# Moving the item product from GpSimd to VectorE and setting the AUGRU widths step by step, in a two-pass recurrent recommendation kernel

## The chip, the cores and the metric

The kernel runs on one NeuronCore of one Trainium2 chip. The metric is the device time of one launch in microseconds (us), the median of several runs. The engines are called as the profile calls them: PE is TensorE, DVE is VectorE, ACT is ScalarE, POOL is GpSimd, and SP is SyncE, which issues most of the DMAs. A matrix product on PE is preceded by a weight load, which the profile lists apart as PEld.

## The reference

There are 1024 items (`B`), 100 steps (`T`) and vectors of 128 numbers, all float32. A GRU runs over the history of every item; an attention network scores each hidden state against the item's embedding; the softmax over the steps pools the hidden states; a second recurrence, the AUGRU, runs over the hidden states with gates that the pooled values scale; and its output at the item's last step goes into a small network.

```python
def gru_step(h, x_t):                                   # 100 steps, all 1024 items
    r = sigmoid(i_r + h_r); z = sigmoid(i_z + h_z)      # i = x Wih' + bih, h = h Whh' + bhh
    n = tanh(i_n + r * h_n)
    return (1 - z) * n + z * h
keys = gru_seq                                          # (1024, 100, 128)
feat = concat([keys, q, keys - q, q * keys])            # q is the item's embedding
score = mlp(feat, [80, 40, 1], relu); score[mask != 1] = -inf
attn = softmax(score, axis=1)
pooled = einsum('bt,btd->bd', attn, keys)
att_seq = pooled.T[:T]
def augru_step(h, (x_t, a_t)):                          # x_t = keys[:, t], a_t = att_seq
    r = sigmoid([h, x_t] Wr' + br); u = a_t * sigmoid([h, x_t] Wu' + bu)
    h_hat = tanh([h * r, x_t] Wh' + bh)
    return (1 - u) * h + u * h_hat
attention_feature = aug_out[item, sequential_length - 1]
out = mlp([user, item, hist_sum, item * hist_sum, attention_feature], [200, 80, 1], sigmoid)
```

`hist_sum` is the masked sum of the history divided by the length. `sequential_length` is drawn uniformly from 1 to 100. Only the AUGRU output at the last step of an item is used, so an item needs no AUGRU step beyond its length.

## The kernel before

**Layout.** Hidden states lie with the 128 features on the partitions and the items on the free axis. The items are cut into two halves of 512 (`HB`), and everything is done half by half, so that one half's chain of elementwise work lies beside the other half's matrix products. A float32 product of 128x512 is two PE instructions in the trace.

**First phase (`gru_phase`).** A loop over the 100 steps; at each step, for each half: load the inputs of two steps ahead (`load`, `load_mask`; the tiles `x` and `m` have 8 buffers each), the GRU step (`gru`, lines 354 to 398), the attention of the previous step (`attend`, lines 418 to 435), the transposition of the previous hidden state for the keys in memory (`transpose`), one stage of the softmax if a block of steps is complete (`stage`), the masked history sum (`history`, lines 350 and 351) and up to two additions to the pooled sum (`pool`, lines 511 to 526). After the second half, `attend_more` does the second and third attention layers of both halves (`px`, lines 618 and 627).

The work lies on the engines so. PE: for each half and step, the gates (`ps`, line 363, 12 instructions), the first attention layer (`pm`, four instructions: line 431 with the hidden state `hn`, line 432 with the product `kq` of `hn` and the item's embedding), and four transposes (`pk`, line 409). DVE: the elementwise chain of the GRU, `u` (383), `ps` plus `u` (393), `d` (396, 397), `hn` (398), and the sum `f` of `pm` and a constant (434). ACT: the sigmoids and tanh (375, 380, 394), the copy of the transposed keys (410), the ReLUs (435, 627). POOL: the item product `kq` (429), the history (`xm`, `hist`) and the pooled sum (`kw`, `pooled`, with the softmax weights `e`).

The tiles `pm`, `pk`, `px` and `pt` (the transposed scores) share two PSUM buffers in turn, so `px` needs the buffer that `f` sets free.

**Order.** The order of the instructions on each engine is fixed when the kernel is built: a scheduler places every instruction by its own estimate of when its inputs are ready, and each engine then runs its list strictly in that order. What stands in the list behind a waiting instruction waits too.

**Between the phases.** The items are ranked by their lengths (`rank`), and sorted weights and row numbers are made, so that in the second phase the items stand in order of falling length, alternating between the halves. In the first phase the kernel also counts how many items are alive at each step (`count`) and compares this with a table of widths: `over` tells whether an item would fall outside it.

**Second phase (`augru_phase`).** The 100 AUGRU steps, for each half six products with 128 columns of weights (lines 725 and 727), three activations, five DVE operations (735 to 745) and the transposition of the key (`pk`, 714, one instruction for each 128 items), all on the first `w` items of the half only. The keys come by indirect DMAs in quarters of four steps (`load_rows`, `G = 4`). `widths` holds one width for each of the 25 groups of four steps: `RAGGED`, 512 for the first three groups and then falling by 21 per group to 52. If `over` is 1 the phase runs with `FULL`, 512 everywhere. The program holds both versions one after the other, and every engine branches on `over`. When a block of 128 items falls out of the width, `predict` computes its outputs, and an indirect DMA writes them.

Of the kernel before, what the change touches and what calls it, by code (L numbers as in the profile page):

```python
# [18 lines left out]
P = 128  # L19
B = 1024  # L20
T = 100
HB = 512
NH = B // HB
NG = B // P
GH = HB // P
# [16 lines left out]
G = 4  # L42
NQ = T // G
# [1 line left out]
AHEAD = 2  # L45


FULL = [HB] * NQ
TOP, FALL = 556, 21
RAGGED = [min(HB, TOP - FALL * q) for q in range(NQ)]  # L50


@with_exitstack
def kernel(ctx: ExitStack, tc: tile.TileContext, a: dict, out: bass.AP):
# [16 lines left out]
    nc = tc.nc  # L71
# [6 lines left out]
    over_d = dram.tile([1, 1], I32, name="over_d")  # L78
# [31 lines left out]
    def load_rows(q, i, widths):  # L110

        r = mid.tile([P, GH, G * P], F32, tag="once", name="rows") if q == 0 else (
            rows["pool"].tile([P, GH, G * P], F32, name="rows")
        )
        for g in range(-(-widths[q] // P)):
            gather(r[:, g, :], keys_d[q], g, i)
        rows[q, i] = r

    def gru_phase(pools):
# [58 lines left out]
        def load_later():  # L178
# [26 lines left out]
                out=alive,  # L205
# [16 lines left out]
            room_i = pre.tile([1, NQ, G], I32, name="room_i")  # L222
            nc.gpsimd.iota(
                room_i, pattern=[[-2 * FALL, NQ], [0, G]], base=2 * TOP, channel_multiplier=0
            )
            room = pre.tile([1, T], F32, name="room")
            nc.vector.tensor_copy(room, room_i.rearrange("o q g -> o (q g)"))
            nc.vector.tensor_scalar_min(room, room, float(B))
            nc.vector.tensor_tensor(out=room, in0=count, in1=room, op=ALU.is_gt)
            over = pre.tile([1, 1], F32, name="over")  # L230
            nc.vector.tensor_reduce(over, room, AX.X, ALU.max)
            over_i = pre.tile([1, 1], I32, name="over_i")
            nc.vector.tensor_copy(over_i, over)
            nc.sync.dma_start(out=over_d, in_=over_i)
            yield

# [78 lines left out]
        class Half:  # L315
# [102 lines left out]
            def attend(self, t):  # L418

                i = self.i  # L420
                mv = wp.tile([P, HB], F32, name="mv", bufs=4)
                self.old, self.mv = self.mv, mv
                if t == T:
                    nc.gpsimd.memset(mv, 0.0)
                if t >= T:
                    return
                h = self.h[t]
                kq = wp.tile([P, HB], F32, name="kq")
                nc.gpsimd.tensor_mul(kq, h, item[:, self.cols])  # L429
                p = pa.tile([P, HB], F32, tag="a", name="pm")  # L430
                nc.tensor.matmul(p, lhsT=wk[i], rhs=h, start=True, stop=False)  # L431
                nc.tensor.matmul(p, lhsT=wkq[i], rhs=kq, start=False, stop=True)  # L432
                f = wp.tile([P, HB], F32, name="f")
                nc.vector.tensor_add(f, p, q0[:, self.cols])  # L434
                nc.scalar.activation(mv, f, AF.Relu)
# [246 lines left out]
            half.features()  # L682
        sort_weights()
        for i in range(NH):
            load_rows(0, i, FULL)

    def augru_phase(pools, widths):

# [8 lines left out]
        rows["pool"] = kp  # L697

        def load_att(t, i):
            w = widths[t // G]  # L700
            at = wp.tile([P, HB], F32, name="at", bufs=6)
            nc.sync.dma_start(
                out=at[:, :w], in_=att_d[i][t, :w].partition_broadcast(P)
            )
            att[t, i] = at

        def load_key(t, i):

            q, n = divmod(t, G)
            w = widths[q]  # L710
            r = rows[q, i]
            p = pa.tile([P, HB], F32, tag="a", name="pk3")
            for g in range(-(-w // P)):
                nc.tensor.transpose(p[:, ts(g, P)], r[:, g, ts(n, P)], ident)  # L714
            k = wp.tile([P, HB], F32, name="k3", bufs=6)
            nc.scalar.copy(k[:, :w], p[:, :w])
            keys[t, i] = k

        def step(t, i):
            w = widths[t // G]  # L720
            k, at, h = keys.pop((t, i))[:, :w], att.pop((t, i))[:, :w], h3[i][:, :w]

            def gate(m, v, name):
                p = ps.tile([P, HB], F32, tag="g", name=name)[:, :w]
                nc.tensor.matmul(p, lhsT=m[:, 1, :], rhs=k, start=True, stop=v is None)
                if v is not None:
                    nc.tensor.matmul(p, lhsT=m[:, 0, :], rhs=v, start=False, stop=True)
                return p

            r = None  # L730
            if t:
                pr = gate(wr, h, "pr")
                r = wp.tile([P, HB], F32, name="r3")[:, :w]
                nc.scalar.activation(pr, pr, AF.Sigmoid, bias=later["br"])
                nc.vector.tensor_mul(r, h, pr)
            pu = gate(wu, h if t else None, "pu")
            nc.scalar.activation(pu, pu, AF.Sigmoid, bias=later["bu"])
            u = wp.tile([P, HB], F32, name="u3")[:, :w]
            nc.vector.tensor_mul(u, pu, at)
            ph = gate(wh, r, "ph")  # L740
            nc.scalar.activation(ph, ph, AF.Tanh, bias=later["bh"])  # L741
            if t:
                nc.vector.tensor_sub(ph, ph, h)  # L743
                nc.vector.tensor_mul(ph, u, ph)
                nc.vector.tensor_add(h, h, ph)
# [51 lines left out]
        for t in range(T):  # L797
            q, n = divmod(t, G)
            for i in range(NH):
                if n == 0 and 0 < q < NQ - 1:  # L800
                    load_rows(q + 1, i, widths)
                if t + 2 < T:
                    load_att(t + 2, i)
                if t + 1 < T:
                    load_key(t + 1, i)
                step(t, i)
            if n == G - 1:
                left = widths[q + 1] if q + 1 < NQ else 0
# [7 lines left out]
    over = nc.values_load(over_d, min_val=0, max_val=1)  # L816
    with tc.If(over > 0) as more:
        with ExitStack() as pools:
            augru_phase(pools, FULL)
    with more.Else():  # L820
        with ExitStack() as pools:
            augru_phase(pools, RAGGED)


# [64 lines left out]
```

## Time and profile before

| | us |
|---|---|
| median of 3 runs | 2664.23 (2659.52 to 2665.18) |
| profiled execution | 2684.05, its span 2681.6 |
| first phase: first `hn` to the start of the last | 15.5 to 1870.3 |
| second phase: first transposition of keys | 1932.5 |
| PE busy in the span | 2434.5 (91%) |
| POOL, DVE, ACT busy | 1370.2, 1382.1, 1215.7 |

A row of instruction groups gives the line, the engine, the operation and its tiles, the form, the count, the busy time and the mean of one in ns, and then the idle time of the engine ahead of these instructions with what ended it. A row of the timeline gives start and duration in us and, in brackets, the idle time of that engine just before with what ended it; `x2` means that two neighbours are merged into one row, so that the duration is that of both. The duration of a PE instruction contains its passage through the array; instructions that follow one another closely overlap, so what a step costs on PE is read from starts and not from durations.

### The profile page before, as it was taken

The numbers are of one execution on the slowest core, as the hardware profiler recorded it, in microseconds if no ns is written. First come the engines' busy times: TensorE is split into PE (matmuls) and PEld (weight loads), VectorE is DVE, ScalarE is ACT, GpSimd is POOL, SyncE is SP. The second block draws the span as 40 slices with busy tenths as digits, with TensorE's granted clock in tenths as the row PEclk, the third lists the DMA queues.
The fourth block names the chain that finished last, engine by engine and source line by source line (L and its number), as shares of the span: only waits on it lengthen the run. The fifth ranks groups of instructions, "written<-read, shape, count | busy, mean of one in ns | idle before, by whom it ended". The sixth has DMA issues, their size and how long they took to land. (4 is left out here: it accounts for less than half of the span.)

```text
span 2681.6 us, 25839 instructions
## 1 busy us (share of the span) xinstructions
PE 2434.5 (91%) x7688; PEld 1232.2 (46%) x7688; DVE 1382.1 (52%) x2530; ACT 1215.7 (45%) x2125; POOL 1370.2 (51%) x1215
## 2 busy tenths in 40 slices
PE   8999888898888888899888888897789999999998
PEld 3443333343333333344333333333444555667887
DVE  6644444544444444545444444454356666666664
ACT  3544444444444444444444444443234444455554
POOL 3457877565656767665656767667512111211220
PEclk9999999999999999999999999998799999999998
DMA  6323322212222222112222222111223233333331
GB/s 141 99 81 97 95 90 66 74 58 73 77 73 76 75 74 75 52 61 73 74 77 73 77 73 77 49 64 36 86 80 108 85 101 98 93 92 96 79 86 23
DMA packets 141655, 210.20 MB, mean 78 GB/s; under 512 B 29646, under 2 KB 75698, under 8 KB 141506
## 3 DMA queue, kind: packets, MB, share of 16 engines
q1 hardware_dynamic: 129410, 170.93, 20.7%
q0 software_dynamic: 12096, 37.54, 4.9%
q8 instruction: 62, 1.02, 0.2%
q14 instruction: 87, 0.71, 0.1%
HBM read 154.12 MB, written 53.87 MB: 78 GB/s over the span
## 5 line engine op out<-in xcount | busy, mean ns | idle before, releaser
L363 PE MATMUL ps<-x,wih 128*128 128x512 f32 x1200 | 603.2, 613 | 4.6 <-DMA x<-in_hist_x 4.6
L363 PE MATMUL ps<-hn,whh 128*128 128x512 f32 x1188 | 594.4, 609 | 0.0
L429 POOL TENSOR_TENSOR kq<-hn,item 128x512 f32<-128x512 f32 x200 | 254.5, 1278 | 559.1 <-DVE hn L398 540.5
L432 PE MATMUL pm<-kq,wkq 128*128 128x512 f32 x400 | 239.6, 684 | 190.2 <-POOL kq L429 190.1
L383 DVE SCALAR_TENSOR_TENSOR u<-ps,bhh,r 128x512 f32<-128x512 f32 x198 | 148.6, 750 | 506.2 <-ACT r L375 309.6
L101 POOL DMA_INDIRECT rows<-keys_d,idx x140 | 132.8, 949 | 535.9 <-PE pk L714 490.4
L363 PEld LDWEIGHTS ps<-hn,whh 128*128 128x128 f32 x1188 | 223.1, 195 | 326.8 <-issue 319.6
L410 ACT COPY kt<-pk 128x512 f32<-128x512 f32 x200 | 117.3, 586 | 517.2 <-PE pk L409 515.7
L363 PEld LDWEIGHTS ps<-x,wih 128*128 128x128 f32 x1200 | 221.7, 199 | 199.3 <-issue 197.9
L394 ACT ACTIVATE ps<-ps,bih 128x512 f32<-128x512 f32 x200 | 132.4, 662 | 321.6 <-DVE ps L393 317.9
L351 POOL TENSOR_TENSOR hist<-hist,xm 128x512 f32<-128x512 f32 x200 | 251.8, 1274 | 1.6
L434 DVE TENSOR_TENSOR f<-pm,q 128x512 f32<-128x512 f32 x200 | 136.7, 684 | 215.1 <-PE pm L432 215.0
L526 POOL TENSOR_TENSOR pooled<-pooled,kw 128x512 f32<-128x512 f32 x190 | 242.3, 1275 | 4.3
L350 POOL TENSOR_TENSOR xm<-x,m 128x512 f32<-128x512 f32 x200 | 229.4, 1162 | 22.9 <-DMA x<-in_hist_x 16.7
L432 PEld LDWEIGHTS pm<-kq,wkq 128*128 128x128 f32 x400 | 79.5, 210 | 300.1 <-POOL kq L429 223.6
L431 PE MATMUL pm<-hn,wk 128*128 128x512 f32 x400 | 206.9, 599 | 6.0 <-ACT kt L410 3.7
L396 DVE TENSOR_TENSOR d<-hn,ps 128x512 f32<-128x512 f32 x198 | 136.0, 687 | 138.5 <-ACT ps L394 137.6
L525 POOL TENSOR_TENSOR kw<-kt,e 128x512 f32<-128x512 f32 x190 | 196.8, 1052 | 1.7 <-DVE old L492 0.4
L409 PEld LDWEIGHTS pk<-ident,hn 128*128 128x128 f32 x800 | 112.6, 155 | 125.8 <-issue 116.8
L627 ACT ACTIVATE mv<-px,bx 41x512 f32<-41x512 f32 x202 | 137.9, 683 | 68.4 <-PE px L618 65.8
L375 ACT ACTIVATE r<-ps,brz 128x512 f32<-128x512 f32 x200 | 137.5, 688 | 67.7 <-PE ps L363 64.6
L743 DVE TENSOR_TENSOR ph<-ph,h 128x512 f32<-128x512 f32 (+22 forms) x198 | 94.6, 478 | 142.4 <-ACT ph L741 127.5
(139 smaller groups left out, 3608.7 us busy)
## 6 DMA issues: line engine op xcount, KB each, us to landing
x<-in_hist_x SPq DMA_DIRECT2D x212, 256.0 KB
keys_d<-kt SPq DMA_DIRECT2D x50, 1024.0 KB
m<-mask_d SPq DMA_DIRECT2D x200, 128.0 KB
at<-att_d SPq DMA_DIRECT2D x22, 256.0 KB
s_b<-mv SPq DMA_DIRECT2D x200, 2.0 KB
rows<-keys_d,idx POOLq DMA_INDIRECT x140
at<-att_d SPq DMA_DIRECT2D x8, 246.5 KB
at<-att_d SPq DMA_DIRECT2D x8, 236.0 KB
```

The costliest lines, as they stand in the source:

```text
L350: nc.gpsimd.tensor_mul(d, x, m)
L351: nc.gpsimd.tensor_add(acc, acc, d)
L363: nc.tensor.matmul(p, lhsT=w[:, g, :], rhs=v, start=(j == 0), stop=(j == len(parts) - 1),)
L375: nc.scalar.activation(r, pr, AF.Sigmoid, bias=brz[:, 0:1])
L383: nc.vector.scalar_tensor_tensor(out=u, in0=ph, scalar=bhh[:, 2:3], in1=r, op0=ALU.add, op1=ALU.mult,)
L429: nc.gpsimd.tensor_mul(kq, h, item[:, self.cols])
L431: nc.tensor.matmul(p, lhsT=wk[i], rhs=h, start=True, stop=False)
L432: nc.tensor.matmul(p, lhsT=wkq[i], rhs=kq, start=False, stop=True)
L434: nc.vector.tensor_add(f, p, q0[:, self.cols])
L525: eng.tensor_mul(d, k, w)
L526: eng.tensor_add(acc, acc, d)
L627: nc.scalar.activation(half.mv[r, :], p[r, :], AF.Relu, bias=bx[r, :])
```

## The change

The item product goes from `nc.gpsimd` to `nc.vector`. The width is looked up for each step and no longer for each group of four. There are three tables in place of two: a tight one, a wider one, and full width. In the tight one the width is 512 up to step 2 and then falls by 5.125 a step (rounded up to an even number) to 16; in the wider one it is 512 up to step 8 and falls in the same way to 46. The sum of the widths over the 100 steps is 30124 before, 26908 in the tight table and 29740 in the wider one. `over` is now 0, 1 or 2, the number of tables that some step does not fit, and the program holds three versions of the second phase behind two branches.

```diff
-FULL = [HB] * NQ
-TOP, FALL = 556, 21
-RAGGED = [min(HB, TOP - FALL * q) for q in range(NQ)]
+EIGHTH, FALL = 8, 41
+SPARE = (10, 40)
+ROOM = [[EIGHTH * (HB + n) - FALL * t for t in range(T)] for n in SPARE]
+WIDTHS = [[min(HB, 2 * -(-r // (2 * EIGHTH))) for r in room] for room in ROOM] + [[HB] * T]
...
-        for g in range(-(-widths[q] // P)):
+        for g in range(-(-widths[q * G] // P)):
             gather(r[:, g, :], keys_d[q], g, i)
...
+            over = pre.tile([1, len(SPARE)], F32, name="over")
+            for j, n in enumerate(SPARE):
+                room_i = pre.tile([1, T], I32, name="room_i")
+                nc.gpsimd.iota(
...
+                nc.vector.tensor_copy(room, room_i)
+                nc.vector.scalar_tensor_tensor(
...
+                nc.vector.tensor_reduce(over[:, j : j + 1], room, AX.X, ALU.max)
+            nc.vector.tensor_add(over[:, 0:1], over[:, 0:1], over[:, 1:2])
...
-                nc.gpsimd.tensor_mul(kq, h, item[:, self.cols])
+                nc.vector.tensor_mul(kq, h, item[:, self.cols])
...
-            w = widths[t // G]
+            w = widths[t]
...
-            if n == G - 1:
-                left = widths[q + 1] if q + 1 < NQ else 0
-                for g in range(GH):
-                    if left <= g * P < widths[q]:
-                        for i in range(NH):
-                            predict(g, i)
+            left = widths[t + 1] if t + 1 < T else 0
+            for g in range(GH):
+                if left <= g * P < widths[t]:
+                    for i in range(NH):
+                        predict(g, i)
...
-    with tc.If(over > 0) as more:
+    over = nc.values_load(over_d, min_val=0, max_val=len(SPARE))
+    with tc.If(over < 1) as fits:
+        augru(WIDTHS[0])
+    with fits.Else():
+        with tc.If(over < 2) as fits:
+            augru(WIDTHS[1])
+        with fits.Else():
+            augru(WIDTHS[2])
```

The lines below the tables stand one to sixteen lines later in the changed file; the same instruction is line 429 before and 441 after, for instance.

On POOL, in the middle of the first phase, this stood in the list of before. `e` are the softmax weights of a block, `kw` and `pooled` the pooled sum, `xm` and `hist` the history, `kq` the item product.

```order
L429 TENSOR_TENSOR kq<-hn,item 128x512 x6
L511 TENSOR_TENSOR pooled<-pooled,e 128x512
L525 TENSOR_TENSOR kw<-kt,e 128x512 x2
L526 TENSOR_TENSOR pooled<-pooled,kw 128x512 x2
L350 TENSOR_TENSOR xm<-x,m 128x512 x2
L351 TENSOR_TENSOR hist<-hist,xm 128x512 x2
L525 TENSOR_TENSOR kw<-kt,e 128x512 x2
L526 TENSOR_TENSOR pooled<-pooled,kw 128x512 x2
L350 TENSOR_TENSOR xm<-x,m 128x512 x2
L351 TENSOR_TENSOR hist<-hist,xm 128x512 x2
L525 TENSOR_TENSOR kw<-kt,e 128x512
L429 TENSOR_TENSOR kq<-hn,item 128x512
```

Six products stood in a row, then a whole block of pooling and history, and the seventh product behind it. In the changed list of POOL this place reads:

```order
L523 TENSOR_TENSOR pooled<-pooled,e 128x512
L537 TENSOR_TENSOR kw<-kt,e 128x512 x2
L538 TENSOR_TENSOR pooled<-pooled,kw 128x512 x2
L362 TENSOR_TENSOR xm<-x,m 128x512 x2
L363 TENSOR_TENSOR hist<-hist,xm 128x512 x2
L537 TENSOR_TENSOR kw<-kt,e 128x512 x2
```

The products are gone from it, and the rest of the order is nearly the same. On DVE, in the first phase, one half's turn was this before:

```order
L398 TENSOR_TENSOR hn<-ps_4879,d 128x512
L383 SCALAR_TENSOR_TENSOR u<-ps_4929,bhh,r 128x512
L393 TENSOR_TENSOR ps_4931<-ps_4931,u 128x512
L396 TENSOR_TENSOR d<-hn,ps_4931 128x512
L397 TENSOR_TENSOR d<-ps_4933,d 128x512
L398 TENSOR_TENSOR hn<-ps_4931,d 128x512
```

and in the changed list the end of one turn and the start of the next, with a stage of the softmax (`e`, `top`) in it, is this:

```order
L410 TENSOR_TENSOR hn<-ps_4830,d 128x512
L446 TENSOR_TENSOR f<-pm,q_173 128x512
L441 TENSOR_TENSOR kq<-hn,item 128x512
L487 TENSOR_TENSOR e<-pt,on 128x4x8
L488 TENSOR_REDUCE top<-e 128x4
L490 TENSOR_TENSOR top<-top 128x4
L491 TENSOR_TENSOR e<-top 128x4
L492 TENSOR_TENSOR e<-e,top 128x4x8
L395 SCALAR_TENSOR_TENSOR u<-ps_4883,bhh,r 128x512
```

The product now stands between `f` and the `u` of the other half. At the end of the second phase's first version, DVE has these rows before:

```order
L744 TENSOR_TENSOR ph<-u_17147,ph 128x512
L745 TENSOR_TENSOR h_1_99<-h_1_99,ph 128x512
L817 UNCONDITIONAL_BRANCH
L739 TENSOR_TENSOR u_17384<-pu,h_0_98 128x512
L747 TENSOR_TENSOR h_0_98<-u_17384,ph 128x512
```

and these in the changed list:

```order
L756 TENSOR_TENSOR ph<-u_16921,ph 128x16
L757 TENSOR_TENSOR h_1_99<-h_1_99,ph 128x16
L832 UNCONDITIONAL_BRANCH
L835 COMPARE_AND_BRANCH
L751 TENSOR_TENSOR u_17033<-pu,h_0_98 128x512
```

The version that stands first behind the branch was the full width (its last step is 512 wide); now it is the tight table (its last step is 16 wide). The first phase's list on PE, some 2060 rows, is the same but for one row.

More of the change, by code (lines that the diff above doesn't have):

```diff
@@ L221, in load_later @@
                 )
[L222 to L231, printed above, removed]
+            over = pre.tile([1, len(SPARE)], F32, name="over")
+            for j, n in enumerate(SPARE):
+                room_i = pre.tile([1, T], I32, name="room_i")
+                nc.gpsimd.iota(
+                    room_i,
+                    pattern=[[-NH * FALL, T]],
+                    base=NH * EIGHTH * (HB + n),
+                    channel_multiplier=0,
+                )
+                room = pre.tile([1, T], F32, name="room")
+                nc.vector.tensor_copy(room, room_i)
+                nc.vector.scalar_tensor_tensor(
+                    out=room,
+                    in0=count,
+                    scalar=float(EIGHTH),
+                    in1=room,
+                    op0=ALU.mult,
+                    op1=ALU.is_gt,
+                )
+                nc.vector.tensor_reduce(over[:, j : j + 1], room, AX.X, ALU.max)
+            nc.vector.tensor_add(over[:, 0:1], over[:, 0:1], over[:, 1:2])
             over_i = pre.tile([1, 1], I32, name="over_i")
-            nc.vector.tensor_copy(over_i, over)
+            nc.vector.tensor_copy(over_i, over[:, 0:1])
             nc.sync.dma_start(out=over_d, in_=over_i)
@@ L684, in gru_phase @@
         for i in range(NH):
-            load_rows(0, i, FULL)
+            load_rows(0, i, WIDTHS[-1])
     def augru_phase(pools, widths):
@@ L709, in load_key @@
             q, n = divmod(t, G)
-            w = widths[q]
+            w = widths[t]
             r = rows[q, i]
@@ L719, in step @@
         def step(t, i):
-            w = widths[t // G]
+            w = widths[t]
             k, at, h = keys.pop((t, i))[:, :w], att.pop((t, i))[:, :w], h3[i][:, :w]
@@ L806, in augru_phase, with augru @@
                 step(t, i)
-            if n == G - 1:
-                left = widths[q + 1] if q + 1 < NQ else 0
-                for g in range(GH):
-                    if left <= g * P < widths[q]:
-                        for i in range(NH):
-                            predict(g, i)
+            left = widths[t + 1] if t + 1 < T else 0
[3 more added lines that the diff above has]
+                        predict(g, i)
     with ExitStack() as pools:
         gru_phase(pools)
-    over = nc.values_load(over_d, min_val=0, max_val=1)
-    with tc.If(over > 0) as more:
+    def augru(widths):
         with ExitStack() as pools:
[L819 to L822, printed above, removed]
+            augru_phase(pools, widths)
+    over = nc.values_load(over_d, min_val=0, max_val=len(SPARE))
[6 more added lines that the diff above has]
+            augru(WIDTHS[2])
 def _laid_out(np, r):
```

## The prediction

> **What bounds the kernel now.** I first read the page's engine shares, then its groups.
>
> ```profile
> span 2681.6 us, 25839 instructions
> PE 2434.5 (91%) x7688; PEld 1232.2 (46%) x7688; DVE 1382.1 (52%) x2530; ACT 1215.7 (45%) x2125; POOL 1370.2 (51%) x1215
> ...
> L429 POOL TENSOR_TENSOR kq<-hn,item 128x512 f32<-128x512 f32 x200 | 254.5, 1278 | 559.1 <-DVE hn L398 540.5
> L432 PE MATMUL pm<-kq,wkq 128*128 128x512 f32 x400 | 239.6, 684 | 190.2 <-POOL kq L429 190.1
> ```
>
> PE carries both phases. Its one large idle time is the 190.1 us ahead of `pm`, line 432, for which POOL's item product is named; POOL itself idled 540.5 us waiting for `hn` ahead of that product. So POOL is not short of time: its list is in a bad order. The waits say how often, and the tile `hn` how long the phase is:
>
> ```profile
> PE pm L432 <- POOL kq L429: 190.1, 38, 7.5
> ```
>
> ```profile
> L398 DVE TENSOR_TENSOR hn<-ps,d x200: 671/692/694, 15.5 to 1870.3; 128x512 f32<-128x512 f32 x100
> ```
>
> 38 waits of up to 7.5 us; 1854.8 us for 99 steps, 18.7 us a step. The timeline of PE shows what a step would cost without them. `px` comes once a step, so the distance of two `px` is a step:
>
> ```profile
> 1015.17 1.06 PE L618 MATMUL px<-mv,w 121*41 121x512 f32 x4
> ...
> 1031.51 1.06 PE L618 MATMUL px<-mv,w 121*41 121x512 f32 x4
> ...
> 1051.48 1.06 PE L618 MATMUL px<-mv,w 121*41 121x512 f32 x4
> ...
> 1063.71 2.07 PE L432 MATMUL pm<-kq,wkq 128*128 128x512 f32 x2 [5.82 <-POOL kq L429]
> ...
> 1073.14 1.02 PE L432 MATMUL pm<-kq,wkq 128*128 128x512 f32 x2
> ...
> 1075.39 1.06 PE L618 MATMUL px<-mv,w 121*41 121x512 f32 x4
> ...
> 1091.19 1.06 PE L618 MATMUL px<-mv,w 121*41 121x512 f32 x4
> ```
>
> A clean step takes 15.80 us (1075.39 to 1091.19), one with a transposition of scores 16.34 (1015.17 to 1031.51), one with a wait of 5.82 us 23.91. The last is 8.11 over the clean one, 2.29 more than it waited: after the gap the pair of `pm` takes 2.07 us in place of 1.02, so the array runs at half speed for a while.
>
> The cause stands in POOL's timeline:
>
> ```profile
> 1025.65 1.06 POOL L511 TENSOR_TENSOR pooled<-pooled,e 128x512 f32<-128x512 f32 x1 [1.07 <-ACT e L485]
> 1026.67 2.05 POOL L525 TENSOR_TENSOR kw<-kt,e 128x512 f32<-128x512 f32 x2
> ...
> 1035.96 2.06 POOL L525 TENSOR_TENSOR kw<-kt,e 128x512 f32<-128x512 f32 x2
> ```
>
> Pooling and history run without a gap from 1025.65 to 1038.02 and on; the next product stands behind them, and PE waits.
>
> **Part 1: the product leaves POOL.** In the changed order no PE instruction of the loop waits for POOL's list. 99 steps of 15.80 are 1564 us, and 28 transpositions of scores (30 blocks in `ENDS`, two of them after the loop) at 0.54 add 15: 1579 against 1854.8, 275 less. About 10 of this is not POOL's: early on DVE waits for the lengths.
>
> ```profile
> 45.29 0.69 DVE L240 CAST order<-len_r 128x1024 f32<-128x1024 int32 x1 [9.55 <-DMA len_r<-in_len_i]
> ```
>
> So 265 us can go. The other way round: 190.1 less 6.34 after the loop (below) is 184 of idle time, and 37 times 2.29 is 85, together 269.
>
> After the last `hn` there is one more such wait, 6.34 us, worth 8.6 with its slow array:
>
> ```profile
> 1880.12 2.07 PE L432 MATMUL pm<-kq,wkq 128*128 128x512 f32 x2 [6.34 <-POOL kq L429]
> ```
>
> **Part 2: the product arrives on DVE.** The nearest row for its price is the same kind of product on DVE, two SBUF inputs of 128x512. Beside it stand three small DVE operations with two SBUF inputs, all of 128x4, at work while POOL did or did not run:
>
> ```profile
> L525 DVE TENSOR_TENSOR kw<-kt,e 128x512 f32<-128x512 f32 x8 | 5.5, 685 | 1.2 <-POOL pooled L526 1.2
> ```
>
> ```profile
> 1022.28 0.15 DVE L478 TENSOR_TENSOR top<-top 128x4 f32<-128x4 f32 x1
> ...
> 1025.72 1.01 DVE L492 TENSOR_TENSOR old<-den,e 128x4 f32<-128x4 f32 x1
> ...
> 1026.86 0.87 DVE L493 TENSOR_TENSOR den<-den,old 128x4 f32<-128x4 f32 x1
> ```
>
> 0.15 us with POOL idle, 1.01 and 0.87 with POOL at work: the DVE operation ends when POOL's current instruction ends (1025.72 + 1.01 is 1026.73, POOL's change from `pooled` to `kw`; 1026.86 + 0.87 is 1027.73, the middle of the two `kw`). So a product costs 0.69 us, and up to POOL's longest, 1.28, more: 1.97. How often POOL is at work follows from 150 us of the loop, 8 steps at 18.7:
>
> ```profile
> 1017.00:1167.00 150.00, 134.65 (x361) 58.83 (x360) 71.35 (x114) 67.50 (x103) 95.57 (x82) 0.93 0.22 71
> ```
>
> 95.57 us of POOL less 16 products of 1.28 are 75, of 8 steps of 15.9: 59%. The mean product should be about 0.69 + 0.6 x 0.64 = 1.1.
>
> The Trainium skill (GPSIMD Engine Reference, section Specifications) states that GpSimd's SBUF interfaces are shared with VectorE and contend with VectorE instructions of two SBUF inputs. That rule speaks against this change, and the rows above agree with it; read as one POOL instruction at a time it leaves the sum as it is, read as a lock for a whole run of POOL it is the first rival.
>
> What is behind the product in DVE's list is the other half's `u`. DVE idles ahead of it:
>
> ```profile
> 1078.69 0.75 DVE L383 SCALAR_TENSOR_TENSOR u<-ps,bhh,r 128x512 f32<-128x512 f32 x1 [3.44 <-ACT r L375]
> ...
> 1085.78 0.75 DVE L383 SCALAR_TENSOR_TENSOR u<-ps,bhh,r 128x512 f32<-128x512 f32 x1 [1.92 <-PE ps L363]
> ...
> 1090.38 0.68 DVE L434 TENSOR_TENSOR f<-pm,q 128x512 f32<-128x512 f32 x1
> ```
>
> 3.44 and 1.92 us in turn: the smaller gap holds even the 1.97, to 0.05 us. This cover matters, since `px` needs the PSUM buffer that `f` frees: `f` ends at 1091.06, `px` starts at 1091.19. Whatever delays `u` beyond the gap delays `px` and PE by as much. The product itself has time: the one made at 1007.38 belongs to the `pm` of the next step.
>
> ```profile
> 1007.38 1.28 POOL L429 TENSOR_TENSOR kq<-hn,item 128x512 f32<-128x512 f32 x1 [7.32 <-DVE hn L398]
> ```
>
> ```profile
> 1021.95 1.02 PE L432 MATMUL pm<-kq,wkq 128*128 128x512 f32 x2
> ```
>
> 14.6 us lie between, so a product 2 us late costs PE nothing.
>
> The cover is thinnest where a softmax stage stands in DVE's list: L488, L492 and L493 can cost three times 0.8 us more, 2.4. I take 0.75 us for each of 28 blocks, nearer to the end where POOL is idle because it waits for that same `e`: 21 us, bounds 0 and 67. In the first eight steps DVE also ranks the items; 16 products of 0.69 are at most 11 us there, I take 3, since DVE's 9.55 us wait covers most. POOL's turn after a product waits up to 0.69; nobody on the path waits for POOL.
>
> The wider `over` computation adds four DVE operations and one on POOL. The dearest of the kind is
>
> ```profile
> L227 DVE CAST room<-room_i 1x100 f32<-1x100 int32 x1 | 0.9, 905 | 0.0
> ```
>
> once; it lies in the same DVE gaps, at most 2 us if they are full. I count nothing.
>
> Part 1 and 2 together: 265 + 8.6 - 21 - 3 = 250 us.
>
> **Part 3: the narrower widths.** In the second phase PE is the bound while the widths are large:
>
> ```profile
> 2100.00:2200.00 100.00, 100.00 (x312) 51.69 (x310) 61.44 (x98) 45.13 (x77) 20.95 (x23) 1.00 0.36 107
> ```
>
> PE 100% busy at full clock. What a half-step costs at a width is the distance between its `h` and the next half's:
>
> ```profile
> 1971.66 0.69 DVE L745 TENSOR_TENSOR h<-h,ph 128x512 f32<-128x512 f32 x1
> 1977.25 0.69 DVE L745 TENSOR_TENSOR h<-h,ph 128x512 f32<-128x512 f32 x1
> ```
>
> ```profile
> 2439.49 0.45 DVE L745 TENSOR_TENSOR h<-h,ph 128x283 f32<-128x283 f32 x1
> 2442.69 0.45 DVE L745 TENSOR_TENSOR h<-h,ph 128x283 f32<-128x283 f32 x1
> ```
>
> ```profile
> 2585.10 0.31 DVE L745 TENSOR_TENSOR h<-h,ph 128x157 f32<-128x157 f32 x1
> ...
> 2589.09 0.31 DVE L745 TENSOR_TENSOR h<-h,ph 128x157 f32<-128x157 f32 x1
> ...
> 2626.71 0.25 DVE L745 TENSOR_TENSOR h<-h,ph 128x94 f32<-128x94 f32 x1
> ...
> 2629.93 0.25 DVE L745 TENSOR_TENSOR h<-h,ph 128x94 f32<-128x94 f32 x1
> ```
>
> 5.59 us at 512, 3.20 at 283, 2.00 at 157 and 1.61 at 94 (the last two are half of a pair of half-steps). Per column that is 0.0104, then 0.0095, then 0.0062 us: it flattens. The tight table takes 1976 columns in steps 0 to 59, 644 in steps 60 to 79 (widths 241 to 118) and 596 in the last 20. For both halves: 1976 x 2 x 0.0104 = 41; 644 x 2 x 0.008 = 10; the last 20 steps are at the floor already, 2. Sum 53, bounds 41 (only the large widths) and 67 (0.0104 everywhere). `predict` is called as often as before.
>
> **Part 4: the branches.** Before, every engine jumps over the full-width version to the one that runs; in the changed order the tight one stands right behind the branch, and a jump over two others comes at the end. PE at the start of the second phase:
>
> ```profile
> 1932.50 2.93 PE L714 MATMUL pk<-ident,rows 128*128 128x128 f32 x12 [3.55 <-issue]
> ...
> 1959.91 2.08 PE L727 MATMUL ph<-r,wh 128*128 128x512 f32 x2 [8.83 <-DVE r L735]
> ```
>
> 3.55 us without a wait the profile shows, and 8.83 soon after. Gain at the start 0 to 12.4, cost at the end 0 to 3.55; I take 8.8 - 3.5 = 5. The Trainium skill (Runtime: NRT & Kernel Launch, section Instruction fetch mechanics) says that a taken branch to a target outside the fetched window stalls on a fetch; by it both waits at the start would go, and the sum here would be 9 in place of 5. The 3.55 us agree; whether the 8.83 belong to it no row shows.
>
> **The sum.** 250 + 53 + 5 = 308 off the span of 2681.6 gives 2373.6. The profiled execution took 2684.05, 2.45 more than its span, and the median of the runs is 0.9926 of that: 2376 x 0.9926 = 2359 us.
>
> **Rivals.**
>
> *VectorE gets in only when POOL's run ends; slower than before.* Then a product waits for a run like the one above, over 12.4 us, on average 6.2, whenever POOL runs. Beyond the gaps of 1.92 and 3.44 this is 5.0 and 3.5 us a step, at POOL's 60% some 5 us x 99 = 500 lost against 265 + 67 gained: about 2830. It decides from a mean loss of 3.35 us a step on (332 / 99). Against it: L493 got in between two `kw` that stood back to back. Chance 3%.
>
> *The gap ahead of `u` is full.* If a product costs its whole 1.97 and anything else sits in the 1.92, each step loses about one POOL instruction, 1.28 x 99 = 127 in place of my 24: 2461. For it: the cover is exact only to 0.05 us. Against: the worst case is not the mean. 9%.
>
> *The tight table is not taken.* Then the wider one saves 384 x 2 x 0.0104 = 8 in place of 53, behind one more jump: 2407. The lengths that the reference draws, counted, leave room for 6 items at the tightest step. 3%.
>
> *PE waits for `x` instead*, since POOL's history frees its buffers: half the stalls back, 2490. POOL's list is lighter than before. 2%.
>
> My forecast keeps 83%. Its own bounds are 265 + 8.6 + 67 + 12.4 off (2314) and 265 - 67 - 11 + 41 - 3.5 off (2442); that range takes in the third rival and leaves out the others, 14%. A measurement here tells 0.2%, 5 us, from no change; only the first rival lies on the other side: faster 0.96, same 0.01, slower 0.03.
>
> **What would show it.** Right: the wait of `pm` for the product gone; `hn` first to last about 1600 us; the product at a mean of 1.0 to 1.2 us, never much over 2; no DVE operation over 2 us; half-steps at 283 columns still 3.2 us. Wrong: idle time ahead of `px` by the hundred us (second rival), a mean product over 4 us (first), `h` rows with widths of 46 at the end (third), PE waiting for the DMA of `x` (fourth), or a second phase that shrinks by less than 41.

## The result and the profile after

The changed kernel takes 2354.68 us (median; 2352.89 to 2357.19), the kernel before beside it 2663.4 (2659.52 to 2665.18): a ratio of 0.8843, 95% interval 0.8828 to 0.8859. That is 309 us less; the forecast was 2359, and its sum 308.

The page of the changed kernel, engine shares and groups:

```profile
span 2355.4 us, 25359 instructions
...
PE 2305.8 (98%) x7640; PEld 1194.4 (51%) x7640; DVE 1528.0 (65%) x2733; ACT 1192.8 (51%) x2125; POOL 1165.7 (49%) x1006
...
L523 POOL TENSOR_TENSOR pooled<-pooled,e 128x512 f32<-128x512 f32 x25 | 26.3, 1052 | 460.1 <-ACT e L497 460.1
...
L444 PE MATMUL pm<-kq,wkq 128*128 128x512 f32 x400 | 204.4, 592 | 0.0
L441 DVE TENSOR_TENSOR kq<-hn,item 128x512 f32<-128x512 f32 x200 | 199.4, 997 | 0.9
```

PE went from 91% to 98% busy. The idle time ahead of the second pair of `pm` (432 before, now 444) fell from 190.2 us to nothing, and the product, now DVE's, takes 0.997 us in the mean. POOL still idles 460 us, but ahead of pooling, with no product behind it. How long the phase is, and how the product spreads, stands in the answer for the tile `hn`:

```profile
L410 DVE TENSOR_TENSOR hn<-ps,d x200: 681/691/693, 14.2 to 1621.0; 128x512 f32<-128x512 f32 x100
L441 DVE TENSOR_TENSOR kq<-hn,item x200: 681/734/1786, 15.4 to 1621.7; 128x512 f32<-128x512 f32 x100
```

First `hn` to last: 1606.8 us against 1854.8. Half of the products take 0.73 us or less, the longest 1.79. The timeline of PE, where one `px` comes per step:

```profile
1015.41 1.06 PE L630 MATMUL px<-mv,w 121*41 121x512 f32 x4
...
1031.75 1.06 PE L630 MATMUL px<-mv,w 121*41 121x512 f32 x4
...
1047.55 1.06 PE L630 MATMUL px<-mv,w 121*41 121x512 f32 x4
```

A step with a transposition of scores takes 16.34 us and one without 15.80: the two numbers that the prediction read as clean. Of the ten blocks of eight steps between step 8 and step 88, nine took 127.48 to 128.03 us; 8 x 15.80 + 2 x 0.54 is 127.48. The tenth, near 300 us, took 135.3. DVE's timeline at the place that looked thinnest, a softmax stage while POOL starts its run:

```profile
1025.96 1.01 DVE L504 TENSOR_TENSOR old<-den,e 128x4 f32<-128x4 f32 x1
...
1027.10 0.87 DVE L505 TENSOR_TENSOR den<-den,old 128x4 f32<-128x4 f32 x1
1028.37 0.75 DVE L395 SCALAR_TENSOR_TENSOR u<-ps,bhh,r 128x512 f32<-128x512 f32 x1 [0.39 <-ACT r L387]
...
1033.36 0.98 DVE L441 TENSOR_TENSOR kq<-hn,item 128x512 f32<-128x512 f32 x1
1035.05 0.75 DVE L395 SCALAR_TENSOR_TENSOR u<-ps,bhh,r 128x512 f32<-128x512 f32 x1 [0.71 <-ACT r L387]
```

The small operations cost 1.01 and 0.87 us, as before, and the product 0.98; and still DVE idles 0.39 and 0.71 us ahead of `u`.

The kernel before was profiled in an execution of 2684.05 us, 20 above its median, and the changed kernel at its usual speed, so their spans differ by 326 us where the medians differ by 309. The comparison below therefore uses e9 and e10, in which both kernels were profiled again side by side.

### The profile page after: what moved, and what is told of

Same layout as the page of the kernel before. It is cut to its first block, busy times and chain, and to the rows that moved or that the text cites. A ratio compares the mean times of both kernels' runs of the same rounds, so it can differ in the third digit from the quotient of the medians.

```text
span 2355.4 us, 25359 instructions
## 1 busy us (share of the span) xinstructions
PE 2305.8 (98%) x7640; PEld 1194.4 (51%) x7640; DVE 1528.0 (65%) x2733; ACT 1192.8 (51%) x2125; POOL 1165.7 (49%) x1006
## 3 DMA queue, kind: packets, MB, share of 16 engines
q1 hardware_dynamic: 129410, 167.64, 22.7%
## 4 chain that ended last, share of the span: by engine, by line
PE 88%; POOL 4%; DMA 3%; DVE 2%; ACT 1%; issue 1%; SPq 0%; ACTq 0%; POOLq 0%; DVEq 0%
PE ps L375 38%; PE pm L443 6%; PE pm L444 6%; PE ph L739 4%; PE pr L739 4%; PE pu L737 4%; PE ph L737 4%; PE pu L739 4%; PE pr L737 4%; PE px L630 4%; PE pk L421 3%; PE pk L726 3%; DMA s_b<-mv 2%; POOL pooled L538 1%; POOL kw L537 1%
## 5 line engine op out<-in xcount | busy, mean ns | idle before, releaser
L375 PE MATMUL ps<-x,wih 128*128 128x512 f32 x1200 | 582.5, 595 | 4.0 <-DMA x<-in_hist_x 4.0
L363 POOL TENSOR_TENSOR hist<-hist,xm 128x512 f32<-128x512 f32 x200 | 268.6, 1358 | 2.5
L362 POOL TENSOR_TENSOR xm<-x,m 128x512 f32<-128x512 f32 x200 | 244.3, 1239 | 37.1 <-DMA x<-in_hist_x 32.8
L523 POOL TENSOR_TENSOR pooled<-pooled,e 128x512 f32<-128x512 f32 x25 | 26.3, 1052 | 460.1 <-ACT e L497 460.1
L537 POOL TENSOR_TENSOR kw<-kt,e 128x512 f32<-128x512 f32 x190 | 209.5, 1120 | 1.8 <-DVE old L504 0.6
L444 PE MATMUL pm<-kq,wkq 128*128 128x512 f32 x400 | 204.4, 592 | 0.0
L441 DVE TENSOR_TENSOR kq<-hn,item 128x512 f32<-128x512 f32 x200 | 199.4, 997 | 0.9
L447 ACT ACTIVATE mv<-f 128x512 f32<-128x512 f32 x200 | 126.1, 631 | 101.5 <-DMA s_b<-mv 49.5
L755 DVE TENSOR_TENSOR ph<-ph,h 128x512 f32<-128x512 f32 (+49 forms) x198 | 87.9, 444 | 115.9 <-ACT ph L753 114.9
L405 DVE TENSOR_TENSOR ps<-ps,u 128x512 f32<-128x512 f32 x200 | 140.0, 700 | 20.8 <-DVE u L395 0.5
```

The source lines that it names most:

```text
L362: nc.gpsimd.tensor_mul(d, x, m)
L363: nc.gpsimd.tensor_add(acc, acc, d)
L375: nc.tensor.matmul(p, lhsT=w[:, g, :], rhs=v, start=(j == 0), stop=(j == len(parts) - 1),)
L441: nc.vector.tensor_mul(kq, h, item[:, self.cols])
L537: eng.tensor_mul(d, k, w)
```

## The experiments

The theory: POOL's strict list held the product back, DVE has room for it, and the tables and the jumps add their parts. The rivals: POOL's slow arithmetic was the limit; DVE's room is nearly full; the jump makes the first AUGRU step long. The runs were measured in three sets (e1 to e4, e5 to e8, e9 to e12), each with the kernel before beside them; the expectations call such a set a call. A ratio is always to the kernel before of the same set.

**e1 and e2: each half of the change alone.** e1 is the kernel before with `nc.vector.tensor_mul(kq, h, item[:, self.cols])`; e2 is the changed kernel with the product back on POOL:

```diff
-                nc.vector.tensor_mul(kq, h, item[:, self.cols])
+                nc.gpsimd.tensor_mul(kq, h, item[:, self.cols])
```

> The kernel before, with the item product on VectorE and nothing else changed (widths by groups of four, two versions of the second phase, as before). If the order of POOL's list was what held PE, the first phase must shrink as in the changed kernel, hn first to last about 1607 us in place of 1855, and the second stay at 749: about 256 us off, some 2407. Rival, the shared SBUF interface eats part of it when the rest of the kernel is as before: over 2450.

> The changed kernel with the item product back on POOL: only the widths and the branches are new. If the two parts are independent, the first phase stays at 1855 us between the first and the last hn with 38 waits for POOL, and the second phase takes about 680 in place of 749: some 2594. Rival, the two parts share a saving: under 2570 or over 2620, and then e1 and e2 don't add up to the whole 309.

e1: 2405.09 us, ratio 0.9027 (0.9014 to 0.9041), 259 less than before in the same set (2664.35). e2: 2611.22, ratio 0.9799 (0.9784 to 0.9814), 53 less. Together 312, against 309 for the whole: the parts add up. e2's expectation was 17 us too low: it was read off the first two profiles, whose second phases differ by some 20 us for another reason (see e9). The groups of e1, then of e2:

```profile
L432 PE MATMUL pm<-kq,wkq 128*128 128x512 f32 x400 | 204.3, 592 | 0.0
```

```profile
L444 PE MATMUL pm<-kq,wkq 128*128 128x512 f32 x400 | 240.5, 686 | 188.2 <-POOL kq L441 188.2
```

PE's 190 us wait goes and stays with the engine of the product.

**e7: the product stays on POOL, in another order.** The kernel before; the temporaries of history and pooled sum get a buffer each, and one pooled addition in place of two follows each half:

```diff
-                d = wp.tile([P, HB], F32, tag="kw", name="xm")
+                d = wp.tile([P, HB], F32, name="xm", bufs=1)
...
-                        d = wp.tile([P, GH, P], F32, name="kw")
+                        d = wp.tile([P, GH, P], F32, name="kw", bufs=1)
...
-                half.pool(2, nc.gpsimd)
+                half.pool(1, nc.gpsimd)
```

> The kernel before, with the product still on POOL: the history and the pooled sum get one buffer of their own each in place of two in common, and at most one step is pooled per half-step in place of two, which makes the scheduler spread POOL's work. Runs of 11 and more POOL operations between two products fall from 47 to 24. POOL does the same work at the same speed. If the order was the fault, about half of the stalls go: 2480 to 2580. Rival, POOL is simply too slow for the product: within 1% of before.

2498.57 us, ratio 0.931 (0.9296 to 0.9324): 186 less than the 2684.98 that the kernel before took in this set. Its groups:

```profile
L429 POOL TENSOR_TENSOR kq<-hn,item 128x512 f32<-128x512 f32 x200 | 255.3, 1277 | 48.1 <-DVE hn L398 40.3 <-PE ps L363 5.4 <-DVE e L480 1.8
L432 PE MATMUL pm<-kq,wkq 128*128 128x512 f32 x400 | 213.1, 615 | 37.0 <-POOL kq L429 36.6
```

The product is as slow as before, 1.277 us, and POOL is as busy (1375.0 us against 1370.2), but PE's wait falls from 190 to 37 us and the loop from 1854.8 to 1664.9. Four fifths of the wait went, where the expectation said half. So it was the order of POOL's list that bound the first phase, not POOL's arithmetic: the rival falls.

**e5: POOL without its work.** The changed kernel leaves out the history sum but for step 0, and the pooled sum but for the last eight steps; DVE still makes the product.

```diff
-                nc.gpsimd.tensor_mul(d, x, m)
-                nc.gpsimd.tensor_add(acc, acc, d)
+                if t == 0:
+                    nc.gpsimd.tensor_mul(d, x, m)
+                    nc.gpsimd.tensor_add(acc, acc, d)
...
```

> The changed kernel without POOL's work in the loop: the history sum is left out but for step 0 and the pooled sum but for the last 8 steps, so POOL is idle beside the products. If VectorE waits for POOL's current instruction, the product takes 0.69 us every time in place of 1.0 on average; and if that wait is covered, the loop stays within 10 us of 1607 between the first and the last hn. Rival, the shared interface costs PE something: the loop shrinks by 20 us or more. After the loop less is left to do, so only the loop is compared.

2375.02 us, ratio 0.8847 (0.8831 to 0.8863). The tile `kq`, and the one new wait of PE:

```profile
L443 DVE TENSOR_TENSOR kq<-hn,item x200: 681/681/1581, 15.8 to 1622.2; 128x512 f32<-128x512 f32 x100
```

```profile
139.69 0.56 PE L484 MATMUL pt<-ident,s_b 4*128 4x4 f32 x4 [23.00 <-DMA s_b<-mv]
```

Without POOL's work the product takes 0.681 us as a rule (mean 0.692): the other 0.3 us are contention. Its price in time: eight clean steps take 127.48 us here, ten times over, against 127.48 to 128.03 in the changed kernel. The loop as a whole is no shorter (1606.9), but for a reason of its own: with POOL idle the loads of the mask are let go early, a long run of them stands on SP's queue ahead of the copies of the scores, and PE waits 23.00 us for these, once. That the whole loop came out the same is thus no proof; the clean blocks are.

**e6: the product twice.** DVE makes each product two times.

```diff
-                nc.vector.tensor_mul(kq, h, item[:, self.cols])
+                for _ in range(2):
+                    nc.vector.tensor_mul(kq, h, item[:, self.cols])
```

> The changed kernel with the item product done twice in a row on VectorE. The gap ahead of u is 3.44 and 1.92 us in turn before the change, and one product takes 1.0 of it. Two take 2.0 on average, up to 2.7 where POOL is at work: if the cover is as thin as the prediction says, PE loses 0.1 to 0.8 us in every second half-step: 10 to 60 us over the changed kernel. Rival, the cover is much larger than the gap (PE itself runs ahead): within 5 us of it. Rival, the gap is already full: 100 us or more.

2417.35 us, ratio 0.9003 (0.8989 to 0.9017). The loop takes 1642.2 us, 35 more than the changed kernel's 1606.8. The size was expected, the way was not. First, DVE's room is used up in most turns. DVE and PE of this kernel:

```profile
1057.91 2.66 DVE L442 TENSOR_TENSOR kq<-hn,item 128x512 f32<-128x512 f32 x2
1060.49 0.74 DVE L395 SCALAR_TENSOR_TENSOR u<-ps,bhh,r 128x512 f32<-128x512 f32 x1
```

```profile
1056.30 1.06 PE L631 MATMUL px<-mv,w 121*41 121x512 f32 x4
...
1072.10 1.06 PE L631 MATMUL px<-mv,w 121*41 121x512 f32 x4
```

Here DVE goes from the two products to `u` without idle time, and still the step takes 15.80 us. DVE waits ahead of only 70 of the 198 `u` (180 in the changed kernel), but most steps are as long as before. What is lost is lost in a few places, most of them once in eight steps. PE, DVE, ACT and SP at one of them:

```profile
1106.17 1.06 PE L631 MATMUL px<-mv,w 121*41 121x512 f32 x4 [2.40 <-ACT kt L422]
```

```profile
1102.72 0.75 DVE L395 SCALAR_TENSOR_TENSOR u<-ps,bhh,r 128x512 f32<-128x512 f32 x1 [4.48 <-ACT r L387]
```

```profile
1101.48 0.63 ACT L448 ACTIVATE mv<-f 128x512 f32<-128x512 f32 x1 [5.25 <-DMA s_b<-mv]
```

```profile
SPq L351 <- POOL xm L362: 20.5, 5, 8.2
```

DVE itself idles 4.48 us ahead of `u`: it is not DVE that is late here. ACT is late, since `mv` waits 5.25 us for its buffer, which a copy of a score row on SP's queue must free; that copy stands behind loads of `m` (351), which wait for POOL's `xm`. And POOL's run of 35 instructions is longer beside the second product: from `pooled` to the last `hist` it is 45.06 us here (1050.45 to 1095.51) and 42.94 in the changed kernel (1025.89 to 1068.83). That these 2.1 us come out as 2.3 more on ACT and 2.4 on PE is read from the traces and was not tested by a run. In the changed kernel the same wait of ACT is there and is covered:

```profile
1074.60 0.63 ACT L447 ACTIVATE mv<-f 128x512 f32<-128x512 f32 x1 [2.92 <-DMA s_b<-mv]
```

**e3: the same tables, the tight one behind two jumps.** Only the order of the three versions is turned round:

```diff
-    with tc.If(over < 1) as fits:
-        augru(WIDTHS[0])
...
+    with tc.If(over > 1) as more:
+        augru(WIDTHS[2])
+    with more.Else():
+        with tc.If(over > 0) as more:
+            augru(WIDTHS[1])
+        with more.Else():
+            augru(WIDTHS[0])
```

> The changed kernel with the three versions of the second phase in the other order, full width first and the tight one last, so that every engine jumps twice to get to it and falls out at the end. If the wait of 8.83 us after the start of the second phase before came from the jump, step 1 takes some 22 us again in place of 12 and the end is 3 us shorter: 7 to 12 us over the changed kernel, 2362 to 2367. Rival, that wait came from the DMA traffic of the gathers, which is the same here: no more than 3 us over it.

2365.11 us, ratio 0.888 (0.8867 to 0.8894): 10.4 more than the changed kernel. PE at the start of the second phase:

```profile
1680.94 2.30 PE L726 MATMUL pk<-ident,rows 128*128 128x128 f32 x9 [10.05 <-DMA rows<-keys_d,idx]
```

PE idles 10.05 us ahead of the first transposition, where the changed kernel has no idle time; 1.9 come back at the end, where nothing is left to jump over (13.5 us from the last `h` to the end, against 15.4). The row names a DMA, but the branch instructions of PE's own queue (PEldq; minimum, median and maximum in ns) account for it, here and, in the last row, in e10, the changed kernel again:

```profile
L832 PEldq COMPARE_BRANCH  x1: 4566/4566/4566, 1670.6 to 1670.6; - x1
L835 PEldq COMPARE_BRANCH  x1: 5593/5593/5593, 1675.2 to 1675.2; - x1
```

```profile
L832 PEldq COMPARE_BRANCH  x2: 92/1932/3772, 1669.2 to 2343.5; - x2
```

A branch that jumps holds PE's queue for 4.57 and 5.59 us here; the changed kernel's takes 0.09 us at the start, where it goes straight on, and 3.77 at the end, where it jumps. So jumps do cost, there; but the first AUGRU step takes 11.9 us here, not the 22 of the profile of before. The expectation put the cost at the wrong place.

**e4 and e8: no width under 64, or 96.** The changed kernel's last six steps, with widths of 42 to 16, take 5.42 to 5.05 us each, where 46 columns still took 3.15. Theory: PE runs at half speed there.

```diff
-WIDTHS = [[min(HB, 2 * -(-r // (2 * EIGHTH))) for r in room] for room in ROOM] + [[HB] * T]
+WIDTHS = [[min(HB, max(64, 2 * -(-r // (2 * EIGHTH)))) for r in room] for room in ROOM] + [[HB] * T]
```

> The changed kernel with no width under 64 (only the last 11 steps differ, which get wider). If PE's clock fell to half in the last six steps because the products had become too narrow to keep the array busy, these steps take 3.2 us again in place of 5.2: 10 to 12 us less, about 2343. Rival, the clock fell because of the 0.33 us gap ahead of a transposition, or because of the predict calls at the end: the same 5.2 us, no change or 1 us more.

> The changed kernel with no width under 96 (the last 17 steps get wider). By the prices of the trace a half-step at 94 columns takes 1.61 us and at 46 about 1.58: within 2 us of the same with a floor of 64, if the clock is whole in both; if 64 columns are still too narrow for a whole clock, this one is 5 to 12 us faster than that.

e4: 2340.46 us, ratio 0.878 (0.8768 to 0.8792), 14.2 less than the changed kernel, with more columns to compute (ten steps get wider, and sixteen with a floor of 96; each expectation counts one more). The `predict` calls are the same, so that rival falls. e8: 2368.88, ratio 0.882 (0.8808 to 0.8833), in the set in which the kernel before took 2684.98. Between 64 and 96 that decided nothing.

**e9 to e12: both kernels and both floors in one set.** e9 is the kernel before, e10 the changed one, e11 and e12 the floors of 64 and 96.

> The kernel before, unchanged, to get its profile and that of the changed kernel from one chip. Theory: what differs between the chips lies in the first AUGRU step (11.9 to 12.3 us in four traces of the first chip, 22.2 to 22.7 us in the kernel before and in four traces of the second) and in a few us of the steps behind it, and belongs to the chip, not to the kernel: the first step here is as long as in the changed kernel of the same call, within 1 us, whichever of the two it is, and the loop takes 1854 to 1856 us. Rival (the jump to the branch makes it): the first step is 22 us here and 12 us in the changed kernel of this call.

> The changed kernel, unchanged. Its span is 310 us (plus or minus 4) below that of the kernel before in this call, 250 of it in the loop, if the 326 us between the two profiles first compared hold 16 to 20 us of chip; 322 to 328 below it if they do not. Ratio of the medians 0.882 to 0.886.

> The changed kernel with no tight width under 64 columns, on the same chip as the floor of 96: 14 us (plus or minus 3) under the changed kernel of this call, last five AUGRU steps at 3.2 us each.

> The changed kernel with no tight width under 96 columns. If the clock alone decides, the last steps are at 3.3 us as before and some ten more steps are wider by up to 32 columns: 1 to 4 us over the floor of 64 in this call. If the 11 us between the two floors in the earlier calls were of the kernel and not of the chip, it is 8 to 12 us over.

e9: 2664.43 us (ratio 1.0004, 0.9995 to 1.0013). e10: 2354.49 (0.8839, 0.8825 to 0.8852). Their spans are 2659.4 and 2352.4, 307.0 apart, 250.2 of it in the loop (1853.7 and 1603.5). e9's first AUGRU step takes 12.47 us, e10's 12.32. ACT's timeline there, in the first profile of the kernel before, then in e9:

```profile
1953.01 0.66 ACT L741 ACTIVATE ph<-ph,bh 128x512 f32<-128x512 f32 x1 [5.72 <-remote]
1957.91 0.59 ACT L716 COPY k<-pk 128x512 f32<-128x512 f32 x1 [4.24 <-remote]
```

```profile
1943.72 0.66 ACT L741 ACTIVATE ph<-ph,bh 128x512 f32<-128x512 f32 x1 [1.05 <-PE ph L727]
```

The long first step is ACT's, which waits twice for something that the profile calls `remote`, in a kernel that also runs without it. All four runs of the set of e5 to e8 have the long step (22.2 to 22.7 us), as the first profile of the kernel before has, and none of the other nine traces. It makes 10 of the 20 us; most of the rest lies in later steps of the second phase (steps 60 to 79 take 104.0 us in the first profile and 97.9 in e9). The expectation spoke of the chip, and that falls too: by the chips' numbers those four and e9 to e12 ran on the same one. It goes with the set; what makes it is open.

The floors: e11 2342.62 us (0.8793, 0.8781 to 0.8805), 11.9 under e10; e12 2341.85 (0.8792, 0.878 to 0.8804). 64 and 96 can't be told apart, and the 11 us by which the ratios of e4 and e8 (0.878 and 0.882) differ were the set's, not the floor's. The windows over the last steps, of e10 and of e11 (the PE clock stands behind POOL's column):

```profile
2306.00:2336.00 30.00, 30.00 (x144) 29.91 (x142) 9.86 (x56) 9.74 (x40) 0.00 (x0) 0.50 0.02 4
```

```profile
2303.00:2321.00 18.00, 16.69 (x140) 15.71 (x139) 11.61 (x56) 10.09 (x41) 0.00 (x0) 1.00 0.06 14
```

With the narrow products the granted clock is 0.50 while PE shows no idle time; with the floor it is 1.00, though PE idles 1.31 of 18 us. That confirms that the narrow widths halve the clock. The floor is the version that beats both kernels.

## Why the prediction was right, point by point

The terms, from e9 to e10 (us; the first `hn` came 0.5 later in e10; `first`, line 600 and then 612, is the last PE work ahead of the second phase):

| step of the prediction | forecast | measured |
|---|---|---|
| loop (parts 1 and 2 without the last stall) | -241 | -250.2 |
| last stall (last `hn` to `first`) | -8.6 | -7.0 |
| start of the second phase (`first` to the first transposition) | -8.8 | -3.9 |
| widths | -53 | -49.9 |
| end of the second phase | +3.5 | +3.3 |
| sum | -308 | -307 (span) |

**The cause was right.** `pm` waits no more, e7 shows order and not speed, e1 gives 259 alone; it forecast 250 for parts 1 and 2.

**The product on DVE was right.** Mean 0.997 us where 1.1 was forecast, none over 1.79. The rule of the Trainium skill (GPSIMD Engine Reference, section Specifications), that GpSimd shares SBUF interfaces with VectorE and contends with its instructions of two SBUF inputs, agrees with e5: 0.692 us without POOL's work, 0.997 with it. As a lock for a whole run of POOL, the first rival, it would show products of several us; there is none.

**The softmax term was too large, and another was missing.** 21 us were charged for 28 softmax stages, 3 for the early steps and 10 for the lengths: the loop was to be 34 us over its clean 1579. It is 24 over, and these lie elsewhere. The softmax stages cost nothing that can be seen (nine blocks at 127.48 to 128.03). Some 15 us lie in the last three steps and 7 near 300 us. The changed kernel's SP queue and its waits, then ACT and PE, in the last three steps:

```profile
1588.17 0.32 SPq L561 DMA_DIRECT2D rlen<-rlen_d  x1
1588.58 0.39 SPq L424 DMA_DIRECT2D keys_d<-kt  x1
1589.06 3.73 SPq L457 DMA_DIRECT2D s_b<-mv  x4
```

```profile
SPq L561 <- POOL hist L565: 36.0, 1, 36.0
```

```profile
1594.38 0.63 ACT L447 ACTIVATE mv<-f 128x512 f32<-128x512 f32 x1 [11.15 <-DMA s_b<-mv]
```

```profile
1599.07 1.94 PE L630 MATMUL px<-mv,w 121*41 121x512 f32 x4 [8.30 <-ACT kt L422]
```

SP holds a load of `rlen` for 36 us until POOL's `hist` at line 565 is done; the copies of the score rows stand behind it, `mv`'s four buffers stay taken, ACT waits 11.15 us, and PE 8.30. The rows say it in reverse order: the wait that is named for PE (`kt`) is only ACT's last step. Near 300 us the trace has the same chain: SP waits 15.3 us (three waits) for POOL's `xm`, ACT's `mv` 6.78 for a copy of the scores, PE 3.93. So the step "nobody on the path waits for POOL" failed: SP does, and what queues behind it. In e5, where POOL is idle, these three steps lose 2.8 us in place of 14.9, the block near 300 us nothing. The fourth rival (PE waits for `x`, since POOL frees its buffers) named the right owner of the buffers, but priced it at half the stalls, 131 us; it was 22.

**The cover was larger than it was read.** The prediction held that whatever delays `u` beyond its gap delays `px` and PE by as much, and that 0.05 us was left. e6 contradicts it: the gap is used up in most turns, and most steps still take 15.80 us, or 16.34 with a transposition. How much room there is in all was not measured. The thin reserve is the one through POOL and SP.

**The widths were right.** Steps 0 to 59 gave 39.6 us (41 forecast), steps 60 to 79 8.0 (10), the last twenty 2.2 (2). This last agreement is a chance one: the twenty gained 7.6 in their first fourteen and lost 5.4 in the last six, at half the clock. "At the floor already" missed that narrower can be slower.

**The branches were mis-sized.** Of the 12.4 us at the start, the prediction took the 8.83 and left the 3.55; the runs say the reverse. PE's wait ahead of the first transposition went from 3.71 us (e9) to none (e10), and the start gained 3.9. The 8.83 did not belong to the jump: e9 jumps too, and its first step takes 12.47 us. The cost at the end was right. By the Trainium skill (Runtime: NRT & Kernel Launch, section Instruction fetch mechanics) a taken branch to a target outside the fetched window stalls. The 4.57 and 5.59 us of e3 agree, and the 8.83 were no case of it.

**The scale.** The profile taken for the sum held 20 us that the median does not, and the factor 0.9926 took them off in proportion, from the saving too. 308 off the median of 2664.23 itself would have been 2356, nearer to 2354.68. That the sum of 308 met the 307 so closely is luck: the loop gained 9 more than forecast, and last stall, start and widths 9 to 10 less.

## What to carry to other kernels

POOL idled for 540 us and was still waited for: it had a bad list, not too much work. In such a case move the urgent instruction out of that list (or change the list) before making it faster. When the cover of a moved instruction is judged, the idle time ahead of the next one is not the whole of it, as e6 showed; and follow also what the slower neighbour frees: here POOL's buffers hold SP's queue, and the copies behind it hold ACT. When work is cut by narrowing, look at the granted clock at the narrow end and keep a floor if it drops: it was worth 12 to 14 us here.

## What was not expected of the hardware

PE's clock halves when the products become narrow, though they follow one another without a gap. The timeline of PE in the changed kernel:

```profile
2299.89 0.39 PE L739 MATMUL pu<-h,wu 128*128 128x56 f32 x2
2300.12 0.39 PE L737 MATMUL ph<-k,wh 128*128 128x56 f32 x2
...
2307.11 0.40 PE L737 MATMUL pu<-k,wu 128*128 128x42 f32 x2
2307.34 0.40 PE L739 MATMUL ph<-r,wh 128*128 128x46 f32 x2
...
2308.58 0.47 PE L726 MATMUL pk<-ident,rows 128*128 128x128 f32 x1 [0.33 <-ACT k L728]
...
2309.56 0.63 PE L737 MATMUL pu<-k,wu 128*128 128x42 f32 x2
2309.98 0.63 PE L739 MATMUL pr<-h,wr 128*128 128x42 f32 x2
```

At full clock the next pair starts 0.23 us after one of 42 columns (2307.11 to 2307.34), no sooner than after one of 56 (2299.89 to 2300.12): there is a floor under a pair. From 2309 on the distance is 0.42 to 0.43. It begins behind a wait of 0.33 us, but e11 waits 0.32 us in each of its last three steps at full clock, so the wait alone is not the reason. The Trainium skill (TensorE: Matmul & The Clock Gate, The HAM clock gate) says that the gate follows how busy PE has been; by the records PE is busy all the time here, so the busy share of a profile is not what it follows. That the array stands idle inside that floor, and that this is counted, is argued and not shown. Where the limit lies between 42 and 64 columns was not tried: in e9 the last steps, at 52 columns, ran at 0.50 as well, and in the changed kernel two steps at 52 and 46 still ran at full clock. In e3 the step at 46 columns took 5.00 us, against 3.14 in e10.
